# Storing a slot in 128 pieces of 16 KB instead of 256 of 8 KB, in a per-example matrix product with residual

## The chip, the cores and the metric

The kernel runs on one core of one Trainium2 chip. The metric is the device time in microseconds of one execution. Times before are the median of three runs; the profile is of one further execution.

## The reference

For each of 128 examples, `x[b]` (128 channels by 1024 columns of f32) is multiplied by the weight matrix that its subject index picks from eight, and added to itself:

```python
w = weights[subjects]                       # (128, 128, 128) from (8, 128, 128)
out = jnp.einsum('bct,bcd->bdt', x, w)      # B = 128, C = D = 128, T = 1024
return x + out
```

So 64 MiB are read, 64 MiB are written, and each example needs one 128 x 128 by 128 x 1024 product in f32.

## The kernel before

SBUF holds a ring of `SLOTS = 12` slots in one tensor `x_all`. A slot takes a turn's four examples (`H * G = 4`, two halves of `G = 2`), each 128 partitions by 4 KB, so that one partition of a slot is 16 KB of consecutive bytes and a slot is 2 MB. There are `NT = 32` turns; turn i uses slot `i % 12`.

*Loads.* ACT issues four DMAs of 512 KB for each turn (`load`), each written so that its DRAM side is 32 rows of 16 KB. For turns 12 and later ACT first waits until the store of the turn 12 earlier has landed (`s_slot`). All loads go by ACT's queue, which the profile calls q10.

*Relay.* POOL waits for the landing of a turn's loads and passes it on to PE in `s_ready`.

*Compute.* For each half, PE multiplies two examples into one of the two PSUM tensors `ps[h]` (line 162). DVE adds the 2048 columns of the half to the slot in place (line 174) and counts up `s_added`, then copies the next turn's two weight matrices to where PE reads them (line 153).

*Stores.* SP first waits until the loads of turn 7, the eighth slot, have landed (`AHEAD = 8`). Then it goes through the turns: it waits for `s_added` of the turn's second half and issues one DMA of 2 MB for the slot. The last turn is stored in three: its first half (1 MB), its third example and, at the end of the program, its fourth (512 KB each). All stores go by SP's queue, q1, on which the subject indices and the eight weight matrices (`w_all`) were loaded at the start. Both queues are served by the same 16 DMA engines.

The DRAM side of a store is `out[b+q0 : b+q1]` seen as (d, g, t): for each of 128 partitions, one row of 4 KB in each of the examples. The SBUF side is cut by `store` into pieces of `g` examples of one partition.

Of the kernel before, what the change touches and what calls it, by code (L numbers as in the profile page):

```python
# [30 lines left out]
G = 2  # L31
# [4 lines left out]
SLOTS = 12  # L36
# [15 lines left out]
def transfer(nc, engine, out, in_):  # L52

    later, nc._always_lower_symbolic_ap = nc._always_lower_symbolic_ap, False
    ins, outs = engine.lower_ap_dma(in_), engine.lower_ap_dma(out)
    nc._always_lower_symbolic_ap = later
    return engine.add_instruction(
        mybir.InstDMACopy(  # L60
            name=nc.get_next_instruction_name(),
            engine=engine.engine,
            ins=ins,
            outs=outs,
            mode="Copy",
            cce_op=ALU.bypass,
            queue=QUEUES[engine.engine],
        )
    )
# [3 lines left out]
def kernel(  # L73
# [17 lines left out]
    if room:  # L91
        sbuf("room", C, room // 4)
    x_all = sbuf("x_all", C, SLOTS * H * G * T)
    xs = [
        x_all[:, i * H * G * T : (i + 1) * H * G * T].rearrange("c (q t) -> c q t", t=T)
        for i in range(SLOTS)
    ]
# [34 lines left out]
    def store(i, q0, q1):  # L132
        b = i * H * G
        transfer(
            nc,
            nc.sync,
            out[b + q0 : b + q1].rearrange("g d t -> d g t"),
            xs[i % SLOTS][:, q0:q1, :].rearrange("d (o g) t -> d o (g t)", g=min(G, q1 - q0)),
        ).then_inc(s_slot[i % SLOTS], DMA)

    def subjects_of(i):
# [36 lines left out]
    with tc.tile_critical():  # L178
# [35 lines left out]
        for i in range(NT):  # L214
            for h in range(H):
                if i == NT - 1 or h == H - 1:
                    nc.sync.wait_ge(s_added, i * H + h + 1)
                    store(i, h * G if i == NT - 1 else 0, (h + 1) * G - (i * H + h == NT * H - 1))
# [54 lines left out]
```

## Time and profile before

| | |
|---|---|
| runs (median, lowest to highest) | 323.63 us (323.34 to 323.68) |
| profiled execution | 323.44 us |
| its span | 321.7 us |
| mean granted TensorE clock | 0.884 |
| PE, DVE busy | 244.1 us (76%), 165.7 us (52%) |
| HBM read, written | 67.63 MB, 67.11 MB |
| DMA issues of x_all | 128 of 512 KB, median 10.7 us to landing |
| DMA issues of out | 31 of 2048 KB, median 54.8 us to landing; 1 of 1024 KB; 2 of 512 KB |

The profile's times are in microseconds from the start of the span. PE is the matmul engine, DVE the vector engine, SP and ACT the two engines whose queues issue DMAs here, POOL the relay. "DMA" in a slice or a window is the mean busy share of the 16 DMA engines, GB/s is what they moved. A line such as L162 is a line of the kernel. Packets are what a DMA engine moves in one piece; a semaphore write at the end of a DMA's share on an engine counts as a packet of its own. Of the 16051 packets, 2609 are under 512 B; nearly all of these are such writes.

### The profile page before, as it was taken

To read this page: it belongs to the slowest core of one execution; us is meant where nothing else is said; L and a number is where in the kernel's file an instruction comes from. 1 tells how busy PE (TensorE), PEld (TensorE's weight loads), DVE (VectorE), ACT (ScalarE), POOL (GpSimd) and SP (SyncE) were. 2 spreads that over 40 slices of the span, in tenths; PEclk is the share of its full clock that TensorE was granted. 3 is DMA by queue.
4 is the path that set the end of the run, shared out by engine and by line. 5 is a ranking of instruction groups with operands and counts; after the bars stand their busy time and mean duration, and the time that the engine had idled before them with its cause. 6 is when DMAs were issued, how large, how long until landed. Compare 5 with 4: busy or idle time off the path is not lost. (4 is left out here: it accounts for less than half of the span.)

```text
span 321.7 us, 2380 instructions
## 1 busy us (share of the span) xinstructions
PE 244.1 (76%) x518; PEld 101.0 (31%) x518; DVE 165.7 (52%) x202; POOL 0.2 (0%) x4
## 2 busy tenths in 40 slices
PE   5999999999999999959499684986959779300000
PEld 2434444443444444424143231432423234000000
DVE  2267776777677677736627465371754707500000
POOL 0000000000000000000000000000000000000000
PEclk9799999999999999979879999897998959755555
DMA  7999999999999999999999999999999999999997
GB/s 281 426 428 426 424 424 408 421 437 418 421 438 428 422 418 426 439 427 423 424 418 425 434 435 413 426 433 427 428 418 425 440 417 421 426 430 425 427 428 309
DMA packets 16051, 134.76 MB, mean 419 GB/s; under 512 B 2609, under 2 KB 3634, under 8 KB 3890
## 3 DMA queue, kind: packets, MB, share of 16 engines
q1 hardware_dynamic: 9906, 67.64, 50.1%
q10 hardware_dynamic: 6144, 67.12, 49.6%
q14 instruction: 1, 0.01, 0.0%
HBM read 67.63 MB, written 67.11 MB: 419 GB/s over the span
## 5 line engine op out<-in xcount | busy, mean ns | idle before, releaser
L162 PE MATMUL ps<-x_all,w 128*128 x512 | 239.6, 626 | 30.2 <-PEq L158 27.1
L174 DVE TENSOR_TENSOR x_all<-ps,x_all 128x2048 f32 x64 | 146.7, 2292 | 106.9 <-DVEq L173 106.9
L162 PEld LDWEIGHTS ps<-x_all,w 128*128 128x128 f32 x512 | 99.3, 199 | 170.5 <-issue 169.7
L153 DVE COPY w<-w_all 128x128 f32 x132 | 23.2, 219 | 4.3 <-DMA w_all<-in_L_cond_weights_dram 4.3
L186 PE MATMUL ps<-zeros 128*128 128x512 f32 x6 | 4.4, 897 | 1.7 <-DVE zeros L183 1.7
L186 PEld LDWEIGHTS ps<-zeros 128*128 128x128 f32 x6 | 1.7, 304 | 3.6 <-issue 1.9
L183 DVE MEMSET zeros<- 128x512 f32 x1 | 0.5, 485 | 1.0 <-SPq L178 1.0
L195 DVE TENSOR_SCALAR near<-given 1x128 int32<-1x128 int32 x1 | 0.2, 217 | 0.6 <-DMA given<-in_itok_B_dram 0.6
L199 DVE CUSTOM_DVE_ANT_0 index<-near,wrap 1x256 uint16<-1x256 uint16 x1 | 0.3, 280 | 0.0
L197 DVE TENSOR_SCALAR wrap<-near 1x128 int32<-1x128 int32 x1 | 0.2, 215 | 0.0
L260 POOL MEMSET const-bfloat16-1.0<- 128x1 bf16 x1 | 0.1, 101 | 0.0
L260 POOL MEMSET const-uint8-127<- 128x1 uint8 x1 | 0.1, 101 | 0.0
L260 POOL MEMSET const-float32-0.0<- 128x1 f32 x1 | 0.1, 98 | 0.2 <-issue 0.2
L260 POOL MEMSET const-float32-1.0<- 128x1 f32 x1 | 0.1, 98 | 0.0
L260 DVE BASE_LOAD x1 | 0.0, 21 | 0.1
L193 DVE MEMSET index<- 1x4 int32 x1 | 0.1, 62 | 0.0
## 6 DMA issues: line engine op xcount, KB each, us to landing
x_all<-in_x_dram ACTq DMA_DIRECT2D x128, 512.0 KB, 10.7
out_dram<-x_all SPq DMA_DIRECT2D x31, 2048.0 KB, 54.8
out_dram<-x_all SPq DMA_DIRECT2D x1, 1024.0 KB, 26.0
out_dram<-x_all SPq DMA_DIRECT2D x2, 512.0 KB, 21.0
w_all<-in_L_cond_weights_dram SPq DMA_DIRECT2D x1, 512.0 KB, 5.1
given<-in_itok_B_dram SPq DMA_DIRECT2D x1, 0.5 KB
```

What stands on the lines that cost most here:

```text
L153: copy = nc.vector.tensor_copy(ws[q], w_all[:, bass.ds(subject[q], 1), :])
L162: mm = nc.tensor.matmul(ps[h][:, q % G, t : t + N], ws[q][:, 0, :], x_all[:, bass.ds(at, N)], start=True, stop=True,)
L174: nc.vector.tensor_tensor(mine, ps[h].rearrange("d g t -> d (g t)"), mine, ALU.add).then_inc(s_added, 1)
L183: nc.vector.memset(zeros, 0.0).then_inc(s_zeros, 1)
L186: nc.tensor.matmul(ps[P_SLOTS - 1][:, G - 1, :N], zeros[:, :D], zeros, start=True, stop=True)
L193: nc.vector.memset(index[:, B:], 0).then_inc(s_index, 1)
L195: nc.vector.tensor_scalar(near, given, -S, S - 1, ALU.max, ALU.min).then_inc(s_index, 1)
L197: nc.vector.tensor_scalar(wrap, near, 0, S, ALU.is_lt, ALU.mult).then_inc(s_index, 1)
L199: nc.vector.tensor_tensor(index[:, :B], near, wrap, ALU.add).then_inc(s_index, 1)
L260: nc = _bacc.Bacc("TRN2", target_bir_lowering=False, num_devices=1)
```

## The change

The number of examples of one SBUF piece in `store` becomes all that the store holds. For the 31 full slots that is 4, so that each partition is one piece of 16 KB instead of two of 8 KB. For the stores of the last turn, of two examples and of one, nothing changes. The wait for the eighth slot, the order of the issues and all counts of semaphores stay.

```diff
             out[b + q0 : b + q1].rearrange("g d t -> d g t"),
-            xs[i % SLOTS][:, q0:q1, :].rearrange("d (o g) t -> d o (g t)", g=min(G, q1 - q0)),
+            xs[i % SLOTS][:, q0:q1, :].rearrange("d (o g) t -> d o (g t)", g=q1 - q0),
         ).then_inc(s_slot[i % SLOTS], DMA)
```

## The prediction

> **What bounds the kernel now.** I read the page first. Its slices and its DMA queues:
>
> ```profile
> DMA  7999999999999999999999999999999999999997
> GB/s 281 426 428 426 424 424 408 421 437 418 421 438 428 422 418 426 439 427 423 424 418 425 434 435 413 426 433 427 428 418 425 440 417 421 426 430 425 427 428 309
> ...
> DMA packets 16051, 134.76 MB, mean 419 GB/s; under 512 B 2609, under 2 KB 3634, under 8 KB 3890
> ...
> q1 hardware_dynamic: 9906, 67.64, 50.1%
> q10 hardware_dynamic: 6144, 67.12, 49.6%
> ```
>
> Only the first and last slices are not full. PE is busy 76% and DVE 52%, so the DMA engines set the time: 134.76 MB at 426 GB/s are 316 us of the 321.7. Next, does the rate depend on what is moved? Four stretches by the windows view:
>
> ```profile
> core 0: us, PE busy (x) PEld busy (x) DVE busy (x) POOL busy (x), PEclk, DMA share, GB/s
> 20.00:40.00 20.00, 20.00 (x46) 8.28 (x45) 14.28 (x16) 0.00 (x0) 1.00 1.02 430
> 52.00:92.00 40.00, 40.00 (x91) 16.76 (x91) 28.51 (x34) 0.00 (x0) 1.00 1.01 427
> 270.00:300.00 30.00, 5.91 (x14) 2.27 (x12) 6.78 (x9) 0.00 (x0) 0.63 1.01 426
> 300.00:321.70 21.70, 0.00 (x0) 0.00 (x0) 0.00 (x0) 0.00 (x0) 0.50 0.91 383
> ```
>
> Loads alone in 16 KB packets (20 to 40), both kinds (52 to 92), stores alone in 8 KB packets (270 to 300): 426 to 430 each (the 430 counts packets by their start; shared out over their durations it is 426). So neither direction nor piece size pays by the byte. The last load lands at 267.1 (the trace's landing events); the other 53 us are stores alone, and the last addition is over at 278.4. That long cover of stores is why no latency of PE or DVE shows at the end.
>
> What the change can move is the order of loads and stores. The DMA view of 52 to 92, where both queues always hold work, counts packets (MB and share behind them):
>
> ```profile
> q10 hardware_dynamic: 915, 10.01, 59.1%
> q1 hardware_dynamic: 912, 7.08, 41.9%
> ```
>
> 915 to 912: the 16 engines serve the two queues packet for packet, semaphore writes counted too, however large the packets. On one engine a load of 512 KB is two 16 KB pieces and a semaphore write (q10 has 6144 packets for 128 loads, 48 each, 3 an engine), 10.7 KB a turn; a store of 2 MB is 16 pieces of 8 KB and a semaphore write, 128 KB in 17 turns, 7.5 KB a turn. That gives 59:41 for the loads, as measured. Loads therefore run ahead until all 12 slots are full, near 95 us, and stay ahead.
>
> **The change, part by part.** *Fewer pieces.* The 31 full stores lose 128 packets each, 3968 in all. The packet records have a median of 0.311 us for 8 KB and 0.616 for 16 KB, so two for one saves at most 0.006 us on one of 16 engines: 3968 x 0.006 / 16 = 1.5 us, if those durations were spent one after another. They overlap (DMA share 1.01 to 1.02) and the rates above are equal, so I take 0; the bounds are 0 and 1.5 us of gain. Bytes, issues (34 stores, 128 loads), semaphore counts and the last slot's stores are as before. Nothing moves on SP, ACT, PE, DVE or POOL, and no wait is added.
>
> *The share of the turns.* A full store becomes 8 pieces and a semaphore write: 128 KB in 9 turns, 14.2 KB a turn, against the loads' 10.7. Now stores get 57% and loads 43% of 426: 243 and 183 GB/s. A slot of 2.097 MB takes 8.6 us to store and 11.5 us to load. Stores gain on loads instead of falling behind.
>
> *Does the cover last?* The first store is issued at 44.8 as before, its first packet starts at 49.05 (4.2 us behind loads that are already queued) and slot 8 has landed at 50.1. So slot n lands at 50.1 + 11.5(n-8), and store k ends at 49.05 + 8.6(k+1). Now the computing in between:
>
> ```profile
> 160.69 16.47 PE L162 MATMUL ps<-x_all,w 128*128 x32 [4.23 <-PEq L158]
> 180.19 7.13 PE L162 MATMUL ps<-x_all,w 128*128 x16 [3.04 <-DVE w L153]
> 188.52 7.13 PE L162 MATMUL ps<-x_all,w 128*128 x16 [1.20 <-PEq L158]
> ...
> 259.21 16.70 PE L162 MATMUL ps<-x_all,w 128*128 x32 [4.08 <-PEq L158]
> ```
>
> ```profile
> 265.73 2.29 DVE L174 TENSOR_TENSOR x_all<-ps,x_all 128x2048 f32 x1 [7.80 <-DVEq L173]
> ...
> 269.10 2.29 DVE L174 TENSOR_TENSOR x_all<-ps,x_all 128x2048 f32 x1 [0.81 <-DVEq L173]
> ...
> 272.79 2.29 DVE L174 TENSOR_TENSOR x_all<-ps,x_all 128x2048 f32 x1 [1.13 <-DVEq L173]
> ...
> 276.15 2.29 DVE L174 TENSOR_TENSOR x_all<-ps,x_all 128x2048 f32 x1 [0.81 <-DVEq L173]
> ```
>
> The first column is the start, the bracket the idle time before. Back to back, a slot takes 3.36 + 3.69 = 7.05 us (the spacing of the additions). After 3.04 us or less of idle PE the first addition starts 4.0 us behind the first matmul; after 3.38 or more, 5.5 to 6.5 behind it (259.21 to 265.73 here; 140.58 to 146.28). I take 5.9. So a slot's data is ready 0.3 + 4.0 + 3.36 + 2.29 = 10.0 us after landing with a warm PE and 11.9 with a cold one. From about slot 12 PE has caught up with the loads, and since it idles 4.4 us of 11.5 after a warm slot and 2.5 after a cold one, the two alternate.
>
> Store k can start at 49.05 + 8.6k but has its data, plus 4.2 us of queueing, at about 50.1 + 11.5(k-8) + 11 + 4.2. The lines cross at k = 26. Followed from there: store 26 ends at 281.3, slot 28 has landed at 280.1. Slot 27 (landed 268.6, cold) is ready at 280.5, on the engines at 284.7; for 3.4 us only loads run, and 4.6 MB of them are left. Store 27 runs to 293.3, and 3.05 MB of loads are left. Slot 28 is ready at 290.0, on the engines at 294.3: another 1.0 us of loads alone, 2.6 MB left. Stores 28 and 29 follow, and the last load lands at 302.9 + 1.05 MB / 183 GB/s = 308.6. No time is lost yet: the engines were busy throughout. What is left then is 0.7 MB of store 29 and all of store 30, done at 315.2, and slot 31.
>
> *The exposed tail.* Slot 31's first half has been added at 308.6 + 0.3 + 5.9 + 2.3 = 317.1; from issue to first packet on idle engines takes 1.0 us (first load: issue 0.9, data 1.9), so its 1 MB flows from 318.1 to 320.6, 2.9 us after the engines fell idle. The second half is added at 320.5, flows from 321.5 (0.9 us idle) to 324.0. Before, the last packet ended at 320.3. Sum: +3.7 us on the profiled execution's 323.44 (321.7 of span and 1.7 around it), 327.1; the median of the runs is 0.2 higher, so **327.3 us**.
>
> *Bounds of the tail.* A warm last slot takes 2 us off. At most, the stores have so little lead that slots 30 and 31 are whole when the last load lands: 9.8 us of work against a chain of up to 0.3 + 6.5 + 3.36 + 2.29 + 1 + 2.5 = 16, so 6.2 us, 329.8. At least, three slots and more are left, 15 us of cover, and nothing is lost.
>
> **The rivals.** *The order does not turn.* If a turn weighs something other than packets, or the semaphore writes take no turns, or the 16 KB pieces are cut up on the way (loads pass in whole 16 KB packets, which speaks against it), loads keep half or more of the rate. Eight slots of lead at the first store are then still there at the end: 39 us of stores cover the 16 us chain, 323.6. For it: 912 to 915 was seen with 8 KB against 16 KB only, and the 1024 packets of 512 B of w_all landed by 6.5 us, too early for one at a time against 16 KB. Against it: the exact match at large pieces.
>
> *A turn is a DMA's whole share of an engine.* Then it would be 32 KB against 128 KB before and after, the change would leave the order alone, and the time would be 323.6. But in 52 to 92 the stores would have moved four times what the loads did, and they moved 0.7 times. Chance 0.02.
> [...]
>
> *The shares turn, but the tail stays covered.* My crossing at slot 26 rests on small differences: a longer queue ahead of each store makes the loads end sooner with more than 15 us of stores behind them. 323.6 again.
>
> *Faster.* Larger pieces do cost less, 1.5 us of the store time, and the tail is covered: 322.1. It decides if stores in 16 KB run at over 427 GB/s alone. Against it: loads in such pieces run at 426.
>
> **How the numbers follow.** An exposed tail: 0.77, spread over +0.7 to +6.2 us, likeliest +3.7. Order not turned 0.09, whole shares 0.02, tail covered all the same 0.06: together 0.17 at 323.6. Faster: 0.06. A measurement of this kernel can tell about 0.2%, 0.65 us, from no change; so faster 0.06, same 0.17, slower 0.77. The range takes in no change at its low end and the thinnest cover at its high end: 323.2 to 329.8.
>
> **What would show it.** Right: queue q1 has 5938 packets; in 52 to 92 packets stay one for one but stores move more than loads, about 57:43; the last load lands near 308, not 267; PE and DVE work until about 320; the last slices show DMA gaps of 3 to 4 us in all, and each full load slot no longer waits for an emptied one. Wrong: stores at or under half in 52 to 92, or a last load before about 304, or a rate in mixed stretches other than 426.

## The result, and the profile after

The changed kernel takes 325.95 us (median of 22 runs, 323.28 to 330.24) where the kernel before took 323.68 (22 runs, 323.16 to 324.03): 2.3 us more, and a spread of 7 us in place of 0.9. The measured ratio is 1.0054, 95% interval 1.0031 to 1.0077, some 1.8 us. It leaves out six slow runs of the changed kernel, over 1.5% above its fastest; the profiled one is among them and its trace shows the loss at the end alone, at unchanged DMA rates, so medians of all runs are used below. The profiled execution took 328.97 us, with a span of 327.2.

The page's slices and DMA queues after:

```profile
DMA  7999999999999999999999999999999999999866
GB/s 277 423 429 429 421 421 403 433 421 423 435 425 423 432 425 423 433 427 423 431 425 423 431 429 421 431 429 423 427 431 425 425 433 423 423 433 425 361 256 256
...
DMA packets 12083, 134.76 MB, mean 412 GB/s; under 512 B 2609, under 2 KB 3634, under 8 KB 3890
...
q1 hardware_dynamic: 5938, 67.64, 48.8%
q10 hardware_dynamic: 6144, 67.12, 48.8%
```

q1 has exactly the 3968 packets fewer, and the same bytes. The DMA engines are as full as before in every slice but the last three, which fall to 361, 256 and 256 GB/s: the whole loss lies there. The windows view of the same execution, beginning with the stretches shown of before:

```profile
core 0: us, PE busy (x) PEld busy (x) DVE busy (x) POOL busy (x), PEclk, DMA share, GB/s
20.00:40.00 20.00, 20.00 (x46) 8.30 (x45) 15.21 (x18) 0.00 (x0) 1.00 1.02 429
52.00:92.00 40.00, 40.00 (x92) 16.84 (x91) 29.17 (x34) 0.00 (x0) 1.00 1.00 426
260.00:300.00 40.00, 28.71 (x61) 11.66 (x61) 20.48 (x24) 0.00 (x0) 0.96 1.01 427
300.00:310.30 10.30, 7.90 (x15) 3.06 (x13) 4.72 (x4) 0.00 (x0) 0.83 0.93 395
310.30:327.20 16.90, 8.82 (x16) 3.60 (x16) 5.51 (x9) 0.00 (x0) 0.82 0.59 248
```

The DMA share times the stretch gives the time in work: behind the last landing, at 310.3, 0.59 x 16.9 = 10.0 us of stores lie in 16.9 us. The DMA view of 52 to 92, q10 the loads and q1 the stores (packets, MB, share):

```profile
q1 hardware_dynamic: 659, 9.72, 57.1%
q10 hardware_dynamic: 661, 7.34, 43.4%
```

Still packet for packet, but the stores now move 57% of the bytes: 243 GB/s against 183, as the prediction had it. A store lands every 8.6 us (59.0, 67.6, 76.2 ...), the loads of a slot every 11.5, and the last load lands at 310.3 instead of 267.1.

### The profile page after: what moved, and what is told of

It is laid out like the page before. It is cut to its first block, busy times and chain, and to the rows that moved or that the text cites. A ratio compares the mean times of both kernels' runs of the same rounds, so it can differ in the third digit from the quotient of the medians.

```text
span 327.2 us, 2380 instructions
## 1 busy us (share of the span) xinstructions
PE 258.5 (79%) x518; PEld 106.0 (32%) x518; DVE 165.6 (51%) x202; POOL 0.2 (0%) x4
## 5 line engine op out<-in xcount | busy, mean ns | idle before, releaser
L162 PE MATMUL ps<-x_all,w 128*128 x512 | 253.1, 653 | 59.4 <-PEq L158 53.7
L162 PEld LDWEIGHTS ps<-x_all,w 128*128 128x128 f32 x512 | 104.1, 209 | 209.0 <-issue 208.7
L186 PE MATMUL ps<-zeros 128*128 128x512 f32 x6 | 5.5, 1083 | 1.7 <-DVE zeros L183 1.7
```

The costliest lines, as they stand in the source:

```text
L162: mm = nc.tensor.matmul(ps[h][:, q % G, t : t + N], ws[q][:, 0, :], x_all[:, bass.ds(at, N)], start=True, stop=True,)
L186: nc.tensor.matmul(ps[P_SLOTS - 1][:, G - 1, :N], zeros[:, :D], zeros, start=True, stop=True)
```

## The experiments

Kernels were timed in rounds beside the kernel before, on the same chip; "before" is its median there. "Last landing" is the landing of the last load in a profiled execution, and the chain is from there to the landing of the last store; both come from the trace's landing events.

| kernel | median (lowest to highest), runs | before | last landing | chain |
|---|---|---|---|---|
| before | 323.68 (323.16 to 324.03), 22 | | 267.1 | covered |
| changed | 325.95 (323.28 to 330.24), 22 | 323.68 | 310.3 | 15.9 |
| again | 326.98 (323.27 to 330.07), 12 | 323.58 | 306.9 | 15.9 |
| ahead10 | 323.80 (323.33 to 324.13), 11 | 323.58 | 302.6 | covered |
| hold | 323.57 (323.22 to 323.70), 11 | 323.44 | 295.5 | covered |
| load32k | 371.79 (368.29 to 375.68), 6 | 323.58 | 314.3 | covered |
| load8k_ahead4 | 327.29 (324.65 to 329.40), 6 | 323.44 | 310.8 | 15.9 |
| before_ahead4 | 323.41 (323.25 to 323.97), 11 | 323.44 | 269.1 | covered |
| tail_split | 324.53 (323.57 to 326.47), 12 | 323.44 | 310.4 | 11.7 |
| warm | 325.96 (325.51 to 328.59), 6 | 323.58 | 307.0 | 15.8 |
| short | 324.90 (324.56 to 324.98), 5 | 323.50 | 310.3 | 11.9 |
| short_late8 | 324.57 (323.90 to 328.46), 12 | 323.50 | 306.6 | 14.9 |
| short_late16 | 329.69 (328.55 to 330.55), 5 | 323.50 | 309.9 | 17.9 |

**More lead at the start.**

```diff
-AHEAD = 8
+AHEAD = 10
```

> The changed kernel with the first store behind the tenth slot instead of the eighth. Theory (stores win 57% of the turns, their lead over the last load runs out, the computing of the last slot is exposed): two slots more of lead; slot n lands at 60 + 11.5(n-10), store k starts near 59 + 8.6k, and it meets data that is not ready only where 59 + 8.6k = 60 + 11.5(k-10) + 15, at k = 34, past the last turn. So no tail: 323.5, within 0.5 us, the last load at about 303 with over three slots of stores left, runs close together (within 1 us), and no DMA gap at the end. Rival 1 (16 KB pieces themselves cost time in the stores): no change, median near 326. Rival 2 (the scatter of the runs comes from the piece size or the memory, not from the tail): the runs still spread over 5 us.

Measured 323.80 with 323.33 to 324.13, ratio 1.0008 (0.9999 to 1.0016). The last load landed at 302.6, as expected at 303. Two slots more of lead take away the scatter and all but 0.2 us of the loss, which is within the noise, with 16 KB store pieces throughout, so the pieces are not dear in themselves. Nor are they a gain: this is the changed kernel with its tail covered, and it is not faster than the kernel before.

**The lead given back in the middle.**

```diff
-                    nc.sync.wait_ge(s_added, i * H + h + 1)
+                    nc.sync.wait_ge(s_added, i * H + h + 1 + (2 * H if i == 24 else 0))
```

> The changed kernel with one longer wait in the middle: the store of turn 24 also waits until turn 26 has been added, about 267 instead of 245 by the changed kernel's trace, so that the engines have no store from 257 to about 271. Theory (an engine without a store moves loads, and the pause gives the loads their lead back while there are loads left): loads alone for 14 us, 6 MB, the last load lands near 298 instead of 307 to 310 with four to five slots of stores left; 323.5 within 0.5 us, no scatter. A wait added makes the kernel faster than without it by about 2.3 us. Rival (stores that wait cost their waiting time): slower than the changed kernel by up to 14 us.

Measured 323.57, ratio 1.0002 (0.9994 to 1.0011), scatter 0.5 us. Its windows around the pause, and from the last landing at 295.5 on:

```profile
257.00:270.00 13.00, 13.00 (x30) 5.69 (x31) 8.21 (x10) 0.00 (x0) 1.00 1.01 426
270.00:295.50 25.50, 22.35 (x51) 9.05 (x49) 18.51 (x24) 0.00 (x0) 1.00 1.01 427
295.50:321.70 26.20, 8.72 (x16) 3.60 (x16) 5.12 (x6) 0.00 (x0) 0.70 0.91 386
```

While SP holds store 24 back, the engines stay full at 426 GB/s: they move loads. 26.2 us remain behind the last landing, far more than the chain. An added wait makes the kernel 2.4 us faster than the 325.95 without it. Other places for the pause were not tried; by this account it must lie where loads are left to fill it.

**The same loss without 16 KB stores.** To the kernel before, loads in 8 KB pieces and an early first store; beside it the control with the early store alone.

```diff
-AHEAD = 8
+AHEAD = 4
-ROWS = 4
+ROWS = 2
```

> The kernel before (stores in 8 KB pieces) with loads in 64 pieces of 8 KB and the first store behind the fourth slot. On an engine a load is four pieces and a semaphore write, 6.4 KB a turn, a store 7.5. Theory (packet for packet): stores get 54%, 230 GB/s, loads 196, without any piece of 16 KB; the four slots of lead run out: 29.4 + 9.1k = 30.5 + 10.7(k-4) + 15.2 at k = 16; from there the stores wait for the computing and the last load lands at 305 to 311, so 325 to 328.5, with scatter, while the same kernel with loads in 16 KB (before_ahead4) stays at 323.5. Rival (16 KB store pieces are the cause): no loss.

> The control: the kernel before with the first store behind the fourth slot and nothing else. Theory: loads win 59% of the bytes while both queues hold work and get ahead from any start until the slots are full; last load at 267, 323.6 within 0.3 us. Rival (a small lead at the start is lost time in itself): slower by 1 us or more.

The control took 323.41, ratio 1.0000 (0.9992 to 1.0009), last landing 269.1 against 267.1 with the start behind the eighth slot: with 59% of the bytes, measured in the kernel before, the loads got ahead from either start. With 8 KB loads it took 327.29, with a scatter of 4.8 us in six runs. Its DMA view of 40 to 80 (packets, MB, share):

```profile
q1 hardware_dynamic: 1188, 9.21, 54.6%
q10 hardware_dynamic: 1197, 7.84, 46.8%
```

Packet for packet again, 54:46 as worked out, the last landing at 310.8 and the same 15.9 us behind it. Both sides have pieces of 8 KB here, as both have pieces of 16 KB in the changed kernel, and in both the stores win, because a store has fewer semaphore writes for its bytes. What decides is which queue moves more bytes in a turn, not how large the pieces are.

**Larger load pieces.**

```diff
-ROWS = 4
+ROWS = 8
```

> The changed kernel with the loads in 16 pieces of 32 KB instead of 32 of 16 KB; stores stay at 16 KB. On one engine a load is then one piece and one semaphore write, 16 KB a turn, against the stores' 14.2. Theory (turns go packet for packet): loads get 53%, 226 GB/s, stores 200; the eight slots of lead grow, the tail is covered, 323.6 within 0.5 us and no scatter. Rival 1 (16 KB store pieces are dear in themselves): no change, median near 326. Rival 2 (a turn is a number of bytes, or an engine cuts pieces at 16 KB): the shares stay 57:43 or go elsewhere, and the tail stays near +2 us.

Measured 371.79 us, ratio 1.146, which none of the expectations had. Windows of loads alone (20 to 60) and of both queues (110 to 210), and the DMA view of the latter:

```profile
20.00:60.00 40.00, 35.10 (x73) 14.71 (x74) 20.58 (x25) 0.00 (x0) 0.91 1.02 249
110.00:210.00 100.00, 81.50 (x173) 33.48 (x172) 54.62 (x66) 0.00 (x0) 0.95 1.01 427
```

```profile
q10 hardware_dynamic: 1382, 22.71, 53.6%
q1 hardware_dynamic: 1380, 19.99, 47.0%
```

With both queues full, turns and shares are as expected, 53:47 at 427 GB/s. But loads alone run at 249 GB/s in this form, where 16 KB pieces run at 426; by these rates the first eight slots, 16.8 MB, take 28 us longer to fill. Why the rate is so low, and where the rest of the 48 us goes, stays open. As a test of the total it failed; as a test of the share it holds.

**A shorter chain for the last slot.** The loads of the last turn's halves count on semaphores of their own (`s_tail`), and POOL passes them on one by one:

```diff
+            elif i == NT - 1:
+                for h in range(H):
+                    nc.gpsimd.wait_ge(s_tail[h], DMA * G).then_inc(s_ready, 1)
```

> The changed kernel in which the last turn's first half may be multiplied as soon as its own two loads have landed (semaphores of their own for the two halves of the last turn); before, PE waits for all four. Theory (what is lost is the chain from the last load's landing to the end, about 15.7 us in the two profiles of the changed kernel, less the stores that are left by then): the first half's chain starts two loads, 2.5 to 6 us, earlier and is off the path; from the last landing it is then 0.3 + 3.4 to 5 of multiplying + 2.3 + 1 + 2.5 and the end, 10 to 11.5 us, against the 11 to 12 us of stores that are left. Median 323.5 to 324.2, with far less scatter than 323.3 to 330. Rival (time is lost in the middle, or the store pieces are slower at the end): median stays near 326.

Measured 324.53, above the expected band's 324.2, and scatter of 2.9 us instead of 7. The last load landed at 310.4, just as in the changed kernel's profile, but the end followed 11.7 us later instead of 15.9 and the span was 323.0 instead of 327.2. What remains is PE's:

```profile
299.08 15.88 PE L166 MATMUL ps<-x_all,w 128*128 x32 [2.71 <-PEq L162]
```

That is slots 30 and 31 in one go: the first half of 31 had landed at 304.2, but PE was busy with slot 30 until about 308, when its second half's addition began (308.15). The store of slot 30 was therefore issued only at 310.5, and the DMA share from 310 to 312 was 0.31.

**PE kept warm.**

```diff
+        for _ in range(FILL if h == 0 else 0):   # FILL = 2
+            nc.tensor.matmul(ps[h][:, 0, :N], zeros[:, :D], zeros, start=True, stop=True)
         nc.tensor.wait_ge(s_ready, 1).then_inc(s_ready, -1)
```

> The changed kernel with two matmuls of zeros ahead of each turn's first half, into the PSUM half that the turn then overwrites; PE does them while it waits for the loads. They take 1.8 us, so that PE idles at most 11.5 - 7.05 - 1.8 = 2.7 us in a turn, under the 3.04 us after which it was still quick. Theory (the size of the tail, and the scatter of the runs, come from PE that starts the last slots slowly after a long idle time): first additions follow the landing by about 4.4 us in every turn, the chain behind the last load is 14 us instead of 16, the time falls to 323.6 to 324.5, and runs lie within 1 us. Rival (the scatter comes from the DMA side, PE's start has no part in it): median stays near 326 and runs still spread over 5 us. Second rival (the matmuls of zeros delay the real ones): slower than the changed kernel by up to 1.8 us.

Measured 325.96: no gain in the median, though five of six runs lay within 0.7 us. The theory's premise fell. In its PE timeline (start, duration, what, idle before in brackets):

```profile
246.99 7.13 PE L166 MATMUL ps<-x_all,w 128*128 x16 [2.88 <-PEq L162]
...
258.06 8.82 PE L166 MATMUL ps<-x_all,w 128*128 x16 [2.23 <-PEq L162]
...
281.50 8.83 PE L166 MATMUL ps<-x_all,w 128*128 x16 [2.86 <-PEq L162]
...
300.46 7.03 PE L166 MATMUL ps<-x_all,w 128*128 x16
307.32 1.88 PE L161 MATMUL ps<-zeros 128*128 128x512 f32 x4
309.04 7.03 PE L166 MATMUL ps<-x_all,w 128*128 x16
```

Behind a gap of 2.88 us the slot was fast, behind gaps of 2.86 and 2.23 it was slow. What decides can be read from the granted clock. In all thirteen traces it is 1.0 or 0.5 and changes only on a grid with steps of 3.41 us. Of the 823 steps at full clock, every one with under 1.4 us of matmuls was followed by a step at 0.5, every one with over 1.5 us by another at 1.0. Two pairs of such steps of this run, around the gaps of 2.88 and 2.86 us (columns as above: PE busy stands third, the clock third from the end):

```profile
245.11:248.52 3.41, 1.53 (x4) 0.82 (x5) 0.08 (x1) 0.00 (x0) 1.00 0.93 394
248.52:251.93 3.41, 3.41 (x10) 1.50 (x9) 0.94 (x1) 0.00 (x0) 1.00 1.06 452
279.24:282.65 3.41, 1.15 (x3) 0.68 (x4) 0.48 (x3) 0.00 (x0) 1.00 1.07 452
282.65:286.06 3.41, 3.41 (x5) 1.33 (x4) 0.00 (x0) 0.00 (x0) 0.50 0.96 408
```

The gap of 2.88 us is shared by two steps and left the second 1.53 us of matmuls, and the step behind it had the full clock; that of 2.86 us lies mostly inside one step, left it 1.15 us, and the step behind it had half. The grid begins elsewhere in each execution: counted from the start of the span, its steps lie 0.1, 0.8 and 2.8 us past multiples of 3.41 in the two traces of the changed kernel and in this one.

And at the end, where loads arrive faster, the zeros stand in the way: the last slot landed at 307.0 and its multiplying began at 309.0. The second rival, a delay by the zeros, took what a warm start gave.

**The changed kernel again.**

> The changed kernel once more, for the spread of its runs and the profile of another execution. Theory: runs fall anywhere from 323.3 to 330; the execution profiled differs from the first one (327.2 us of span) only in the last slots: how late after its loads slots 27 to 31 were added, and the DMA gaps after the last load make up the difference to 321.7. Rival: the difference lies in the rate of the DMA engines, spread over the whole span.

Runs from 323.27 to 330.07; the profiled one took 325.55, span 323.8. PE timelines of the end, the first execution's and then this one's:

```profile
280.90 7.13 PE L162 MATMUL ps<-x_all,w 128*128 x16 [2.85 <-DVE w L153]
...
299.07 8.83 PE L162 MATMUL ps<-x_all,w 128*128 x16 [2.73 <-PEq L158]
310.72 8.82 PE L162 MATMUL ps<-x_all,w 128*128 x16 [2.82 <-DVE w L153]
```

```profile
280.42 22.97 PE L162 MATMUL ps<-x_all,w 128*128 x48 [2.03 <-PEq L158]
307.29 8.82 PE L162 MATMUL ps<-x_all,w 128*128 x16 [3.90 <-PEq L158]
```

The chains are the same, 15.9 us. What differs is when the last load lands, 310.3 or 306.9, and that 3.4 us is the difference of the spans. In the first execution slot 28 was done in 7.13 us and its store was issued at 290.6; here it was slower, and the store came at 291.8. Slot 30 had landed at 298.7 there and at 295.9 here. A store that came late while loads were left let loads through and shortened the tail (slot 28's here); one that came late when none were left lengthened it (slot 30's in the first execution, issued at 310.5 behind the last landing at 310.3, with a DMA share of 0.31 from 310 to 312).

The landing events show a second part. Each load has sixteen of them, one an engine, and has landed with the last. In the first execution fifteen had done theirs of the last load by 308.84 and one only at 310.35; here the last four came between 306.72 and 306.92. So 1.5 of the 3.4 us is one engine that trailed the others. Why it did stays open.

**PE taken out.** A quarter of the columns are multiplied; then POOL delays every turn by the same amount:

```diff
-                    ps[h][:, q % G, t : t + N],
+                    ps[h][:, q % G, t : t + SHORT],     # SHORT = 128
-                    x_all[:, bass.ds(at, N)],
+                    x_all[:, bass.ds(at, SHORT)],
...
+                for n in range(PAD):                    # PAD = 8 or 16, none in the first kernel
+                    nc.gpsimd.memset(pad, 0.0).then_inc(s_pad, 1)
+                    late = nc.gpsimd.wait_ge(s_pad, (i - 1) * PAD + n + 1)
+                late.then_inc(s_ready, H)
```

> The changed kernel with a quarter of the product: each matmul takes 128 of its 512 columns, the rest of the PSUM halves holds zeros from the start, so three quarters of the product are left out; loads, additions and stores are whole. PE then needs some 2 us a slot instead of 7.1 or 8.8. Theory (the loss is the chain behind the last load): data is ready about 7 us behind its landing, the chain is about 11 us against 11 to 12 us of stores; 323.3 to 324 without scatter. Rival (the loss comes from the order of DMAs alone): near 326, with scatter.

> As the kernel with a quarter of the product, and POOL clears a small tile eight times between a turn's landing and passing it on, a delay of the same length in every turn (about 3 us by estimate; its profile tells) that takes no time of PE, DVE or DMA engines. Theory: the chain is that much longer, about 14 us, and the loss about 1 to 3 us. If the scatter of the changed kernel comes from PE's uneven speed (7.1 or 8.8 us a slot), runs here lie within 1 us; if it comes from how loads and stores interleave at the end, they scatter by 3 us and more as there.

> The same with sixteen clears, about 6 us by estimate. Theory: the chain is about 17 us, longer than the changed kernel's 15.7; loss 3 to 6 us, 326.5 to 330, more than with eight clears. Scatter as told for eight: under 1 us if PE's uneven speed makes it, 3 us and more if the interleaving does. Rival (the delay is hidden because later stores let loads through earlier): no loss at either delay.

PE now takes the same 3.6 to 3.8 us for every slot late in the run, at a low clock:

```profile
300.00:309.90 9.90, 3.78 (x16) 3.49 (x16) 3.94 (x7) 3.60 (x12) 0.50 0.96 407
309.90:328.80 18.90, 3.62 (x16) 3.44 (x16) 7.36 (x9) 4.98 (x16) 0.59 0.53 225
```

(These are the windows of the kernel with sixteen clears, up to and behind its last landing.) Without delay the chain is 11.9 us and the loss 1.4, where at most 0.5 was expected: at its last landing, 310.3, the stores had 0.7 us of slot 29 and 4.9 us each of slots 30 and 31 left, 10.5 us, and 11.9 - 10.5 is the 1.4. With eight clears, 0.311 us each in the median, PE began 3.4 us behind the landing, the chain is 14.9, and the loss 1.1, at the low end of what was expected; its last load landed at 306.6. With sixteen, PE began 6.3 us behind, the chain is 17.9 and the loss 6.2, just over the 3 to 6 expected. The loss is thus not the chain alone: the middle kernel has a chain 3.0 us longer than the first and loses no more, as its last load landed 3.7 us earlier. Its stores came later and let loads through, but that is not all: with sixteen clears they came later still and the last load landed at 309.9, where fifteen engines had done their share by 307.56 and one trailed. The scatter is 0.4 us in five runs, 0.9 in eleven of twelve (the other at 328.46) and 2.0 in five, against 7 in 22 with PE at two speeds. That points to uneven PE as the larger part of the scatter; the stray run and the 2.0 us show that the last loads and stores make some by themselves. The runs are few, and how much of each falls to a given run stays open.

## Why the prediction was right or wrong

*What bounds the kernel, and where the change acts: right.* Bytes at 426 to 427 GB/s, the same for 8 and 16 KB; one packet in turn from each queue, semaphore writes counted; shares of 57:43; 8.6 us a store; the loss only at the end. The rival that a turn is a DMA's whole share of an engine stays refuted for such pieces: 659 to 661 here, where whole shares would give nine packets of a store to three of a load, and 1382 to 1380 with loads of 32 KB.

*The fewer pieces at nothing: right.* With the tail covered, the changed kernel took 323.80 and 323.57 beside 323.58 and 323.44.

*The crossing at slot 26: right.* Store 26 landed at 282.9 (281.3 was worked out), and store 27 was the first to be late: 293.6, 10.7 us behind it instead of 8.6.

*The chain: right.* The prediction's last packet, at 324.0, lies 15.4 us behind its last landing at 308.6; 15.9 us to the last store's landing were measured in three executions. The 1.0 us from issue to first packet were too few: the 1.9 is the start of a 512 B packet on q1, and the first load's data began at 2.2; the changed kernel's stores issued at 310.46, 318.73 and 322.10 had theirs at 311.65, 319.94 and 323.24, 1.1 to 1.2 us later.

*The size of the exposed tail: wrong, and this is the step that failed.* It was 3.7 us, from a single course of the last five slots: a last landing at 308.6 with 4.9 MB of stores left behind it, 11.5 us of cover for the chain. Two executions had the last load at 310.3 and 306.9, on either side of that, with 4.2 and 5.2 MB left, and lost 5.5 and 2.1 us by their spans. The median of the 22 runs is 2.3 us above the kernel before, that of the twelve later runs 3.4. Taken back through 1.75 us outside the span, 1.0 us behind the last store's landing and the 15.9, the first median stands for a last landing near 307.3, if the chain is the same there. So the term had the landing 1.3 us too late, and every microsecond there is one of the end.

*Why it was mis-sized: one course where the traces show several.* The prediction drew a line between 3.04 and 3.38 us of idle from a handful of rows and let slots alternate by it. Gaps of 2.2 to 2.9 us turned out to go either way, by where they fall on the clock's grid, and each slow slot is ready 1.7 us later. It had stores pause for 3.4 and 1.0 us while loads passed; the pauses, as stretches without a store packet, were 2.2 and 1.2 us in the first execution (282.2 to 284.4, 293.2 to 294.4) and about 2.5 and 2.0 in the second. It took all engines as done with the last load at once, where one trailed by 1.5 us in the first execution. And it took slot 30 as added by the last landing; in the first execution its store was issued at 310.5, and the DMA share from 310 to 312 was 0.31. How much of the 1.3 us each of these makes is not shown.

*The rivals.* "The order does not turn" is refuted by the packet counts. "The shares turn, but the tail stays covered" fits some executions by their times, though none of them was profiled: 6 of the 22 runs lay at 323.9 or below. Its 0.06 was too little as a share of runs. "Faster" found no support: stores alone in pieces of 16 KB ran at 423 GB/s (the kernel with the pause, 297 to 315), against 426 in pieces of 8 KB.

## What to carry to other kernels

Where DMA engines are full and serve two queues packet for packet, as here (915 to 912, 659 to 661, 1188 to 1197, 1382 to 1380), the bytes that each queue moves in a turn are a scheduler: they set which stream wins (the loads with 59% before, the stores with 57% after), and that decides what is left at the end to cover the last computing. Work them out from the pieces, semaphore writes included, and give the stream that must finish first the larger share, or hold the other one back while there is still work to fill the pause. When the cover at the end is about as long as the chain, forecast a spread and not a point.

## What the runs showed of the hardware that was not expected

- Loads in pieces of 32 KB of DRAM, each over eight partitions, ran alone at 249 GB/s; the same loads in pieces of 16 KB over four partitions run alone at 426, and with stores beside them both forms fill the engines at 426 to 427.
- PE's slow slots (8.8 us instead of 7.1) came behind idle gaps of 2.23, 2.86 and 3.90 us, and slots of 7.1 us behind 2.85 and 2.88. The length of the gap alone does not tell; in the thirteen traces the matmul time in a step of the 3.41 us grid does, with the line between 1.4 and 1.5 us. A step need not be idle throughout for the clock to fall: steps with up to 1.49 us of matmuls were followed by the slow clock.
- One of the 16 DMA engines finished its share of the last load 1.4 to 2.4 us behind the other fifteen in five of the traces (1.5 in the changed kernel's first), and a load has landed only when all have.
- A program with no change in its instructions or data had runs from 323.3 to 330.2 us. Two traces of it agree within 0.5 us in the landings of all stores up to slot 26 and part behind that, where stores, loads and slow PE slots meet differently.
